# A four-stage network on one core: k's biases by a transfer of their own, padding zeroed by ScalarE, the recurrence's weights zeroed from the output bias

## The chip, the core and the metric

The kernel runs on one core of one Trainium2 chip. The metric is the time of one execution on the device in microseconds (us), the median of several runs. A profile of one execution lists every instruction with its engine, start and duration: PE (TensorE), DVE (VectorE), ACT (ScalarE), POOL (GpSimd) and SP (SyncE, which here only issues transfers). Line numbers are those of the kernel before.

## The reference, cut to what matters

The input x has shape (16, 512, 256). Four sublayers follow each other, each closed by a residual and a layer norm:

```python
x = layernorm(x + latent_attention(x))   # 16 heads of 16, latent size 32, rotary, causal softmax
x = layernorm(x + fp4_ffn(x))            # 256 -> 704 -> 256; activations and weights quantized
x = layernorm(x + recurrence(x))         # tanh state of 64 per head, 512 steps
x = layernorm(x + mix_ffn(x))            # token shift, sigmoid gate, squared relu

# inside latent_attention
qkv = x @ c_attn_w.T + c_attn_b
q_lat = rope(q @ q2l_w.T + q2l_b)
k_lat = rope(k @ kv2l_w.T + kv2l_b)
v_lat = v @ kv2l_w.T + kv2l_b
att = softmax(causal((q_lat @ wqk_w.T + wqk_b) @ k_lat.T * 32 ** -0.5))
y = (att @ v_lat) @ l2o_w.T + l2o_b
return y @ cproj_w.T + cproj_b
```

All values are float32.

## The kernel before, in words

The first two sublayers are computed together, batch by batch, for 16 batches; then the last two, token by token, in 512 steps. Only the start of the first batch matters here.

A preparation comes first. SP and ACT issue the transfers of weights. POOL makes constants: the identity, `mask` (L367, zeros with a triangle of large values), `ones`. The weights of the q and k heads are transposed by TensorE (L719) and copied into `wqk` (L725) in pieces, by whichever of ACT and VectorE the scheduler picks (`nc.any`). The heads of k are stacked with their two halves exchanged, so their biases are needed with the halves exchanged as well: that is `cabk` (L399), made by two small copies on VectorE.

`heads` (L442, L446) then makes q and k of batch 0, `latents` (L460 to L481) their rotated latents `qc` and `kc` and the product `qr`. In between, `output_weights` (L727 to L773) folds the value path, the output map and their biases into one matrix `wv` and one row `bo`, spread over all partitions: `turned_k`, `turned_o` (L737), `there` (L746), `wv` (L754), `by` (L765), `wide` (L766), `ps_bo` (L770, L771), `bo` (L772). POOL adds `bo` to the residual input of batches 0 and 1 (`load_residual`, L415, eight instructions).

`scores` (L527) makes the products S of a group of four heads, VectorE adds the mask and takes the row's extreme in one instruction (`p`, L539), ACT takes exponentials (L552), TensorE turns p (L562), ACT copies the turned p (L564). `values` (L424) makes v in a padded form, `vpad`: each head's 16 columns stand in 32, with zeros beside them. The zeros are written once, by POOL (L789), and the copies of L430 fill the rest, batch by batch. `weighted` (L593) multiplies.

Beside the attention of batch 0 the weights of the FP4 sublayer are quantized (`ffn_weights`, `fp4`): each tile is loaded by SP (L228) into one of two buffers, and then passes VectorE (L205 to L218, eight instructions) and POOL (L219, L220).

`recurrent_weights` (L109) prepares the third sublayer: it zeroes `wb` and `wc` on POOL (L116, L118), then places the blocks of the recurrence's weights in them by 16 and 4 small transfers (L132, L126), loads `ta` by 8 and takes its tanh on ACT (L135), loads four square matrices (L138) and `bout` (L140), which VectorE halves (L141). It is called in batch 2's turn of the loop, but the scheduler moves its instructions to the start, as nothing holds them.

The order on TensorE is the order in which the code calls it (`manual_schedule`). The order on every other engine and in SP's queue is the scheduler's: it follows priorities and the times at which it expects operands. Each engine runs its list strictly in order, and so does SP: an instruction that waits holds all behind it. Transfers use eight semaphores in turn, so each also waits for the transfer that had the same one.

Of the kernel before, what the change touches and what calls it, by code (L numbers as in the profile page):

```python
# [14 lines left out]
AF = mybir.ActivationFunctionType  # L15
ALU = mybir.AluOpType
# [3 lines left out]
P = 128  # L20
B, T, C = 16, 512, 256
NT = T // P
# [37 lines left out]
def tile_kernel(ctx: ExitStack, tc: tile.TileContext, I: dict, out: bass.AP):  # L60
    nc = tc.nc
# [11 lines left out]
    cols = const.tile([P, NCOLS], F32, name="cols")  # L73
# [32 lines left out]
    own = ctx.enter_context(tc.tile_pool(name="own", bufs=1))  # L106
    sq = {}

    def recurrent_weights():  # L109

        ta = own.tile([P, 2, 4, P], F32, name="ta")
        wb = own.tile([P, 4, 2, 2, P], F32, name="wb")
        nc.gpsimd.memset(wb, 0.0)  # L116
        wc = own.tile([P, 4, 2, 32], F32, name="wc")
        nc.gpsimd.memset(wc, 0.0)  # L118
        for par, quarters in enumerate(QUARTERS):
            for i, (r, c) in enumerate(quarters):  # L120

                e = i % 2
                of, rs, cs = slice(e * 64, e * 64 + 64), slice(r * 64, r * 64 + 64), slice(c * 64, c * 64 + 64)
                nc.sync.dma_start(ta[rs, par, :, cs], I["bda"][of, i // 2 :: 2, of])
                if par == 0:
                    nc.sync.dma_start(  # L126
                        wc[cs, :, r, c * 16 : c * 16 + 16],
                        I["bdc"][of, i // 2 :: 2, e * 16 : e * 16 + 16],
                    )
                for q2 in range(2):  # L130
                    at = slice(q2 * 64 + i * 16, q2 * 64 + i * 16 + 16)
                    nc.sync.dma_start(  # L132
                        wb[at, q2::2, par, r, cs], I["bdb"][at, q2 * 2 + i // 2 :: 4, of]
                    )
        nc.scalar.activation(ta, ta, AF.Tanh)  # L135
        for k in ("woutT", "wrT", "wkT", "wvT"):
            sq[k] = own.tile([P, 2, C], F32, name=k)
            nc.sync.dma_start(sq[k], I[k].rearrange("(n p) c -> p n c", p=P))  # L138
        bout = own.tile([P, C], F32, name="bout")
        nc.sync.dma_start(bout, I["bout"].to_broadcast([P, C]))  # L140
        nc.vector.tensor_scalar(bout, bout, 0.5, None, ALU.mult)  # L141
        return ta, wb, wc, bout
# [139 lines left out]
    def quantize_now(j):  # L282

        for _ in quantize(B - 1, j):
            vector_done(("x", B - 1, j))
# [60 lines left out]
    with ExitStack() as a:  # L346
# [8 lines left out]
        def load(b):  # L355
            xT_of[b] = xin.tile([P, 2, T], F32, tag="xT", name="xT")
            nc.sync.dma_start(xT_of[b], I["xT"][b].rearrange("(n p) t -> p n t", p=P))
# [8 lines left out]
        mask = wts.tile([P, T], F32, name="mask")  # L366
# [18 lines left out]
        bo = wts.tile([P, C], F32, name="bo")  # L385
# [5 lines left out]
        for i in range(2):  # L391
            nc.gpsimd.tensor_copy(bd["bdqs"][:, i::2], bd["bdq"][:, 1 - i :: 2])
            at = COLS["q2lb"][0]
            nc.sync.dma_start(q2lbs[i::2, :], I["cols"][1 - i :: 2, at : at + 1])

        cabk = wts.tile([P, 2], F32, name="cabk")
        for i in range(2):
            at = COLS["cab"][0] + 2
            nc.vector.tensor_copy(  # L399
                cabk[i * 64 : i * 64 + 64, :], cols[64 - i * 64 : 128 - i * 64, at : at + 2]  # L400
            )

        vpad = [wts.tile([P, NT, H, 32], F32, name=f"vpad{i}") for i in range(2)]
# [7 lines left out]
        def load_residual(b):  # L411
            x = xres.tile([P, NT, C], F32, tag="x", name="x")
            nc.sync.dma_start(x, I["x"][b * T : b * T + T, :].rearrange("(n p) c -> p n c", p=P))
            for j in range(NT):
                nc.gpsimd.tensor_tensor(x[:, j, :], x[:, j, :], bo, ALU.add)  # L415
            x_of[b] = x
# [102 lines left out]
        def scores(b, g, n):  # L519

            q, k = stack_of[b, g]
            S = [mm("S") for _ in range(4)]
            for i, at in BLOCKS[n]:
                w = (i + 1) * P
                for h in range(4):
                    rs = slice(h * 32, h * 32 + 32)
                    nc.tensor.matmul(  # L527
                        S[h][:, at : at + w], q[rs, i * P : i * P + P], k[rs, :w],
                        start=True, stop=True,
                    )  # L530
            if n == 0:
                sum_of[b, g] = small.tile([P, 2, 2, 4], F32, tag="sm", name="sm", bufs=3)
            tiles = []
            for h in range(4):
                p = pp.tile([P, T], F32, tag="p", name="p")
                nm = small.tile([P, 2], F32, tag="nm", name="nm", bufs=10)
                for u, (i, at) in enumerate(BLOCKS[n]):
                    own = slice(at, at + (i + 1) * P)
                    nc.vector.tensor_tensor_reduce(  # L539
                        out=p[:, own], in0=S[h][:, own], in1=mask[:, T - (i + 1) * P :],  # L540
                        scale=1.0, scalar=-MASKED, op0=ALU.add, op1=ALU.min,
                        accum_out=nm[:, u : u + 1],
                    )
                tiles.append((p, nm))
            return tiles

        def exponentials(b, g, n, h, p, nm):

            for u, (i, at) in enumerate(BLOCKS[n]):
                own = slice(at, at + (i + 1) * P)  # L550
                half, cb = PLACE[i]
                nc.scalar.activation(  # L552
                    p[:, own], p[:, own], AF.Exp, bias=nm[:, u : u + 1], scale=-1.0,
                    accum_out=sum_of[b, g][:, cb, half, h : h + 1],
                )
            return p

        def turn(n, p):
            w = sum(i + 1 for i, _ in BLOCKS[n]) * P
            ps = mm("ps_pt")  # L560
            for at in range(0, w, P):
                nc.tensor.transpose(ps[:, at : at + P], p[:, at : at + P], ident)  # L562
            pT = ptp.tile([P, T], F32, tag="pT", name="pT")
            nc.scalar.copy(pT[:, :w], ps[:, :w])  # L564
            return pT
# [220 lines left out]
        ps_y = five.enter_context(tc.tile_pool(name="ps_y", bufs=1, space=PSUM))  # L786
        banks[:] = [ps_2] * 2 + [ps_b] * 5
        for i in range(2):
            nc.gpsimd.memset(vpad[i], 0.0)  # L789

        with tc.manual_schedule(engines={mybir.EngineType.PE}):
            slots = [(b, g, n) for b in range(B) for g in range(4) for n in range(len(BLOCKS))]
            pTs, before, beside = [], None, None

            behind = []
            for slot in slots + [None]:
                if slot:
                    b, g, n = slot
                    if g == 0 and n == 0:
                        if beside:  # L800
                            beside.rest()
                        if b + 1 < B:
                            load(b + 1)
                        beside = Beside(b)
                        if b == 2:
                            ta, wb, wc, bout = recurrent_weights()
                    if g == 3 and n == 0:
                        load_residual(b)
                    tiles = scores(b, g, n)
                ps = []  # L810

                for h in range(4):
                    beside.half_slot()
                    if before:
                        pTs.append(turn(before[0][2], before[1][h]))
                    if slot:
                        behind.append((*slot, h, *tiles[h]))
                        ps.append(tiles[h][0])
                    while len(behind) > (LAG if slot else 0):
                        exponentials(*behind.pop(0))  # L820
                    if h == 1:
                        divide()
                    beside.half_slot()
                if before and before[0][2] == len(BLOCKS) - 1:
                    weighted(*before[0][:2], pTs)
                    pTs = []
                before = (slot, ps) if slot else None
            divide()
            last_projection = out_projection(B - 1)
            next(last_projection)  # L830
            quantize_now(0)
            next(last_projection)
# [297 lines left out]
    with tc.manual_schedule(engines={mybir.EngineType.PE}):  # L1130
# [40 lines left out]
        for t in range(T):  # L1171
# [9 lines left out]
            for g in range(2):  # L1181
                if us[g] is None or us[g][0] + us[g][1] == t:
                    t0, n = starts[g].pop(0)
# [9 lines left out]
            if t % 8 == 7:  # L1193
                at = t % 16 - 7
# [113 lines left out]
```

## Time and profile before

| what | value |
|---|---|
| runs | 2535.84, 2541.34, 2544.07 us |
| median | 2541.34 us |
| the profiled execution's time | 2540.61 us |
| its span, first to last instruction | 2538.8 us |
| mean granted TensorE clock | 0.982 of full speed |
| the recurrence's first product (L1029) starts at | 1813.2 us |

The profile's rows name the line, the engine, the operation, and output and inputs by the program's names. "Idle before" is the time for which the engine had nothing to run ahead of that instruction, with the instruction or transfer that ended the wait behind an arrow. The granted clock is the share of its full clock that TensorE was given in a stretch. The first ten microseconds are filled by transfers (249 GB/s in that stretch); TensorE starts at 6.1 us with the transposes.

### The profile page before, as it was taken

To read this page: it belongs to the slowest core of one execution; us is meant where nothing else is said; L and a number is where in the kernel's file an instruction comes from. 1 tells how busy PE (TensorE), PEld (TensorE's weight loads), DVE (VectorE), ACT (ScalarE), POOL (GpSimd) and SP (SyncE) were. 2 spreads that over 40 slices of the span, in tenths; PEclk is the share of its full clock that TensorE was granted. 3 is DMA by queue.
4 is the path that set the end of the run, shared out by engine and by line. 5 is a ranking of instruction groups with operands and counts; after the bars stand their busy time and mean duration, and the time that the engine had idled before them with its cause. 6 is when DMAs were issued, how large, how long until landed. Compare 5 with 4: busy or idle time off the path is not lost.

```text
span 2538.8 us, 73782 instructions
## 1 busy us (share of the span) xinstructions
PE 2405.2 (95%) x28802; PEld 1710.4 (67%) x28802; DVE 1925.8 (76%) x5479; ACT 1621.0 (64%) x5536; POOL 1044.4 (41%) x1646
## 2 busy tenths in 40 slices
PE   8789999999999999999999999987799999999997
PEld 4555666666666666666666666655578888888885
DVE  5767888788888888888888888877656666666666
ACT  4656666676766767666666666654366666666664
POOL 4323333333333333333333333333545555555554
PEclk9889999999999999999999999999899999999999
DMA  4000000000000000000000000000111111111100
GB/s 118 24 9 6 12 24 14 16 16 12 24 14 16 16 12 24 14 16 16 12 24 14 16 14 6 16 14 9 43 32 41 41 36 41 41 40 37 36 28 27
DMA packets 58015, 61.30 MB, mean 24 GB/s; under 512 B 7873, under 2 KB 53058, under 8 KB 57666
## 3 DMA queue, kind: packets, MB, share of 16 engines
q1 hardware_dynamic: 56802, 55.54, 7.0%
q8 instruction: 226, 3.70, 0.6%
q10 hardware_dynamic: 864, 1.05, 0.1%
q14 instruction: 123, 1.01, 0.1%
HBM read 39.79 MB, written 16.78 MB: 22 GB/s over the span
## 4 chain that ended last, share of the span: by engine, by line
PE 52%; DVE 28%; ACT 10%; POOL 5%; issue 4%; DMA 0%; DVEq 0%; POOLq 0%; ACTq 0%
PE u L1069 8%; DVE p L539 5%; PE ps_pt L562 5%; PE u L1029 5%; ACT p L552 4%; PE S L527 3%; PE ps_d L164 3%; DVE q_q L210 3%; PE pg L164 3%; PE pu L164 3%; PE ps_h L442 3%; ACT pT L564 3%; DVE q_q L218 2%; DVE q_sc L205 2%; PE ps_a L909 2%
## 5 line engine op out<-in xcount | busy, mean ns | idle before, releaser
L552 ACT ACTIVATE p<-p,nm 128x512 f32<-128x512 f32 (+3 forms) x1024 | 570.3, 562 | 492.0 <-DVE nm L539 488.0
L1077 ACT ACTIVATE hist<-u 64x64 f32<-64x64 f32 x2048 | 447.2, 218 | 233.9 <-PE u L1069 149.6
L539 DVE CUSTOM_DVE_ANT_0 p<-S,mask 128x512 f32<-128x512 f32 (+3 forms) x1024 | 442.7, 483 | 52.6 <-PE S L527 52.1
L562 PEld LDWEIGHTS ps_pt<-ident,p 128*128 128x128 f32 x2560 | 301.7, 142 | 217.0 <-issue 105.9
L1069 PEld LDWEIGHTS u<-hist,ta 128*64 128x64 f32 x8176 | 366.8, 138 | 118.6 <-ACT hist L1077 40.3
L564 ACT COPY pT<-ps_pt 128x384 f32<-128x384 f32 (+1 forms) x768 | 374.1, 517 | 58.0 <-PE ps_pt L562 57.8
L562 PE MATMUL ps_pt<-ident,p 128*128 128x128 f32 x2560 | 395.6, 280 | 4.7 <-DVE nm L539 3.3
L1069 PE MATMUL u<-hist,ta 128*64 128x32 f32 x8176 | 393.4, 218 | 4.6 <-ACT hist L1077 4.5
L219 POOL TENSOR_TENSOR q_q<-q_q,q_m 128x256 f32<-128x256 f32 (+1 forms) x142 | 166.7, 1174 | 368.5 <-DVE q_q L218 366.4
L527 PE MATMUL S<-kc,qr 32*128 32x512 f32 (+3 forms) x2048 | 223.9, 475 | 10.5 <-ACT qr L481 7.9
L1029 PE MATMUL u<-xt,wb 128*64 128x64 f32 x4128 | 224.6, 231 | 5.8 <-issue 5.2
L552 ACT ACTIVATION_READ_ACCUMULATOR p<-p,nm 128x1 f32 x1024 | 199.7, 195 | 0.0
L164 PE MATMUL ps_d<-wdT,hT 128*128 128x256 f32 x732 | 172.8, 386 | 13.7 <-DVE nm L539 12.1
L164 PE MATMUL pg<-wgT,xqT 128*128 128x352 f32 x512 | 177.2, 469 | 7.7 <-DVE nm L539 5.1
L476 POOL TENSOR_TENSOR qc<-qc,qs 128x512 f32<-128x512 f32 x64 | 81.5, 1274 | 232.1 <-DVE qs L475 217.7
L164 PE MATMUL pu<-wuT,xqT 128*128 128x352 f32 x512 | 174.6, 464 | 1.0 <-DVE nm L539 1.0
L1029 PEld LDWEIGHTS u<-xt,wb 128*64 128x64 f32 x4128 | 166.4, 140 | 10.6 <-issue 5.4
L593 PEld LDWEIGHTS py<-pT,vpad 128*32 128x32 f32 x5120 | 139.7, 110 | 47.2 <-issue 30.3
L593 PE MATMUL py<-pT,vpad 128*32 128x128 f32 x5120 | 164.0, 276 | 7.7 <-ACT pT L564 7.5
L164 PEld LDWEIGHTS ps_d<-wdT,hT 128*128 128x128 f32 x732 | 135.1, 191 | 37.1 <-DVE nm L539 15.4
L86 POOL TENSOR_SCALAR ve<-mv 128x2 f32<-128x2 f32 (+1 forms) x160 | 31.1, 195 | 311.7 <-DVE mv L94 309.0
L578 POOL COPY rcx<-rc 128x256 f32<-128x256 f32 x64 | 40.4, 631 | 287.3 <-DVE rc L576 259.5
(164 smaller groups left out, 4645.6 us busy)
## 6 DMA issues: line engine op xcount, KB each, us to landing
xT<-in_xT_dram SPq DMA_DIRECT2D x16, 512.0 KB
x<-in_x_dram SPq DMA_DIRECT2D x16, 512.0 KB
xs<-x SPq DMA_DIRECT2D x64, 128.0 KB
x<-xs SPq DMA_DIRECT2D x32, 256.0 KB
xm<-xs SPq DMA_DIRECT2D x32, 256.0 KB
out_dram<-o SPq DMA_DIRECT2D x64, 128.0 KB
w<-in_w_down_dram SPq DMA_DIRECT2D x2, 352.0 KB
w<-in_w_gate_dram SPq DMA_DIRECT2D x5, 128.0 KB
```

Source lines behind the costliest of these rows:

```text
L164: nc.tensor.matmul(dst, left, right, start=start, stop=stop)
L219: nc.gpsimd.tensor_tensor(q, q, m, ALU.subtract)
L476: nc.gpsimd.tensor_tensor(of[k], of[k], x, ALU.add)
L527: nc.tensor.matmul(S[h][:, at : at + w], q[rs, i * P : i * P + P], k[rs, :w], start=True, stop=True,)
L539: nc.vector.tensor_tensor_reduce(out=p[:, own], in0=S[h][:, own], in1=mask[:, T - (i + 1) * P :], scale=1.0, scalar=-MASKED, op0=ALU.add, ...
L552: nc.scalar.activation(p[:, own], p[:, own], AF.Exp, bias=nm[:, u : u + 1], scale=-1.0, accum_out=sum_of[b, g][:, cb, half, h : h + 1],)
L562: nc.tensor.transpose(ps[:, at : at + P], p[:, at : at + P], ident)
L564: nc.scalar.copy(pT[:, :w], ps[:, :w])
L593: nc.tensor.matmul(py[q * 32 : q * 32 + 32, PLACE[i][1], :], vpad[b % 2][:, j, g * 4 + h, :], pt, start=j == 0 and h % 2 == 0, stop=j == i ...
L1029: nc.tensor.matmul(u[rs, k, par:n:2, bs : bs + 16], wb[:, g * 2 + k, par, half, rs], xt[:, g, at : at + n - par : 2, :], start=par == 0 an ...
L1069: nc.tensor.matmul(into[cs, :, c, :], ta[:, t % 2, g * 2 + k, cs], own[:, :, c, :], start=False, stop=True, skip_group_check=True,)
L1077: nc.scalar.activation(state[g][rs, :, r * 32 : r * 32 + 32].rearrange("p k (s b) -> p k s b", s=2), u[rs, :, t - t0, :] .rearrange("p k ( ...
```

## The change

It has three parts. `cabk` is no longer copied from the loaded `cols` by VectorE, but loaded from memory by two transfers on SP. The zeros of `vpad` are written by ScalarE, as the mask times zero, instead of by POOL. `wb` and `wc` are zeroed on POOL still, but as the output bias `bo` times zero, so that this can't start before `bo` is there; the function gets `bo` for it.

```diff
-    def recurrent_weights():
+    def recurrent_weights(bo):
         ta = own.tile([P, 2, 4, P], F32, name="ta")
         wb = own.tile([P, 4, 2, 2, P], F32, name="wb")
-        nc.gpsimd.memset(wb, 0.0)
+        nc.gpsimd.tensor_scalar(
+            wb.rearrange("p a b c n -> p (a b c n)").rearrange("p (j n) -> p j n", n=C),
+            bo.unsqueeze(1).to_broadcast([P, 8, C]), 0.0, None, ALU.mult,
+        )
         wc = own.tile([P, 4, 2, 32], F32, name="wc")
-        nc.gpsimd.memset(wc, 0.0)
+        nc.gpsimd.tensor_scalar(wc.rearrange("p a b n -> p (a b n)"), bo, 0.0, None, ALU.mult)
...
         cabk = wts.tile([P, 2], F32, name="cabk")
         for i in range(2):
             at = COLS["cab"][0] + 2
-            nc.vector.tensor_copy(
-                cabk[i * 64 : i * 64 + 64, :], cols[64 - i * 64 : 128 - i * 64, at : at + 2]
+            nc.sync.dma_start(
+                cabk[i * 64 : i * 64 + 64, :], I["cols"][64 - i * 64 : 128 - i * 64, at : at + 2]
             )
...
         for i in range(2):
-            nc.gpsimd.memset(vpad[i], 0.0)
+            nc.scalar.activation(
+                vpad[i].rearrange("p j h d -> p j (h d)"), mask.unsqueeze(1).to_broadcast([P, NT, T]),
+                AF.Identity, scale=0.0,
+            )
...
-                            ta, wb, wc, bout = recurrent_weights()
+                            ta, wb, wc, bout = recurrent_weights(bo)
```

With it the scheduler lists some of the first instructions in another order. VectorE makes all eight pieces of `wqk`, `turned_o` and `there`; it runs `qc`, `kc`, `by`, `wide`, `qs` and `ks` ahead of the quantization of the third and fourth weight tile, and that ahead of the first `p`; it halves `bout` ahead of the second group's `qc` and `kc`. POOL's list has `wb` behind the eight additions of `bo` and the third tile's L219, and `wc` behind the fourth's. SP's list has the two `cabk` transfers behind `q2lbs`, the transfers of `ta` ahead of the fifth weight tile, and those of `wc` and `wb` last, behind `bout`. TensorE's list is unchanged.

## The prediction

> **What bounds the kernel now.** I read the page first: the span, the busy shares and the chain that ended last.
>
> ```profile
> span 2538.8 us, 73782 instructions
> PE 2405.2 (95%) x28802; PEld 1710.4 (67%) x28802; DVE 1925.8 (76%) x5479; ACT 1621.0 (64%) x5536; POOL 1044.4 (41%) x1646
> PE 52%; DVE 28%; ACT 10%; POOL 5%; issue 4%; DMA 0%; DVEq 0%; POOLq 0%; ACTq 0%
> ```
>
> TensorE is busy 95% of the span and is over half of the chain. The order of instructions on each engine, before against after, differs only before the second block of softmax work, some 45 us into the span; from there on all five engines run the same list. So the change is worth what it does to the first 45 us, and I read those next, by stages:
>
> ```profile
> 16.20:26.30 10.10, 7.50 (x40) 4.59 (x38) 8.81 (x29) 1.59 (x4) 4.21 (x7) 1.00 0.36 97
> 26.40:36.60 10.20, 9.33 (x19) 3.02 (x20) 2.98 (x9) 4.12 (x11) 7.82 (x10) 0.50 0.21 42
> 36.70:46.70 10.00, 10.00 (x50) 5.85 (x50) 4.45 (x13) 6.88 (x18) 0.00 (x0) 1.00 0.54 162
> ```
>
> The columns are length, busy time of PE, PE's loads, DVE, ACT and POOL, then the granted clock. From 26.4 to 36.6 us TensorE had half its clock. The timeline says why, and names what the change touches:
>
> ```profile
> 3.34 6.06 DVE L399 COPY cabk<-cols 64x2 f32<-64x2 f32 x2
> 3.64 3.56 POOL L789 MEMSET vpad<- 128x2048 f32 x2
> ...
> 7.13 1.81 POOL L116 MEMSET wb<- 128x2048 f32 x1
> ...
> 9.61 0.23 DVE L379 TENSOR_SCALAR w<-w 128x128 f32<-128x128 f32 x1 [0.22 <-DMA w<-in_bdw_dram]
> 9.76 1.20 DVE L725 COPY wqk<-ps_t 128x128 f32<-128x128 f32 x5
> ...
> 11.01 3.78 PE L442 MATMUL ps_h<-xT,wqk 128*128 128x512 f32 x4 [2.95 <-DVE wqk L725]
> ...
> 25.43 1.11 PE L770 MATMUL ps_bo<-cpT,wide 128*128 128x256 f32 x4 [2.12 <-issue]
> ...
> 28.70 5.52 POOL L415 TENSOR_TENSOR x<-x,bo 128x256 f32<-128x256 f32 x8
> ...
> 32.64 0.69 DVE L539 CUSTOM_DVE_ANT_0 p<-S,mask 128x512 f32<-128x512 f32 x1 [5.80 <-PE S L527]
> ```
>
> Each row is start, duration, engine and instruction, then the idle time before it and what ended it. VectorE's tiny cabk copies take 6.06 us while POOL fills vpad and wb; yet VectorE's next instruction waits for w's DMA until 9.61. Later PE idles 2.12 us before ps_bo, because `wide` (L766) stands on VectorE behind the quantization of weight tiles three and four.
>
> **The change, part by part.** All times are worked against the profiled execution: span 2538.8, time 2540.61 us, 1.8 outside the span; that is 0.73 under the median of the three runs (2541.34).
>
> *The cabk copies become transfers.* This takes 6.06 us from VectorE, but w's transfer, issued at 3.16 ahead of the two new ones, still lands at 9.6: VectorE gains its 0.22 of idle at most, nothing on the path. On SP the two narrow transfers stand behind q2lbs; two of that kind took 1.50 us with a wait in them, wb's 0.6 each. Each SP transfer also waits for the one eight places before it, so two more shift every such pairing: cawv now waits for sin (landed about 9.5) instead of cos (8.5) and goes at 9.7 for 8.51; the first weight tile goes at about 11.2 for 10.28. The DMA engines are 0.8 busy to 20 us with the same bytes in the same order, so I take the landings as moved by 0 to 0.9 us, 0.3 likely (first tile 14.2 to 14.5). cabk itself leaves by 9.7 and is used at 17.0: even the 4.1 us of bout (40.74 issued, 44.84 used) leaves 3 us of cover.
>
> *vpad zeroed by ScalarE.* It adds two activations of 128x2048 on ACT. L1014's 128x1024 takes 1.04; between 1.7 and 2.1 each, so some 4 us. ACT is free from its table load (ends 5.55) to its first `heads` at 14.83: hidden with over 4 us to spare. Without that cover the price would be 4 us. In exchange the three L725 copies that ACT made go to VectorE (eight copies, 9.8 to 11.6), but the second is now the last half of the block that PE's first `heads` product needs: PE starts at about 10.35 instead of 11.01. turned_o (0.37) and `there` (0.26) go from ACT to VectorE too, behind the first two tiles' quantization: I put turned_o at 16.2, `there` at 18.0, ps_w at 18.1 (18.61 before): gain 0.5, range 0 to 0.7.
>
> *What VectorE does next.* qc, kc, by, `wide`, qs and ks now stand ahead of tiles three and four. ps_q to ps_ks take PE as long as before, to 22.8. VectorE takes the third tile's maximum at 20.6, after POOL's first wq, qc to 21.6, the fourth maximum at 22.1 (POOL's second wq), kc to 23.2, by and wide 0.6 more: PE's ps_bo at 23.8 instead of 25.43, an idle gap of 1.0 for 2.12. qs and ks end at 25.15. So far the change is 1.6 us ahead.
>
> *What that pushes back.* Tiles three and four (eleven VectorE instructions, some 2.7 us alone) now run after ks and ahead of the first p (L539), while POOL adds qc, kc (1.27 each) and the eight x+bo (0.69 each): continuous from 24.65. Before, they ran in 20.6 to 24.1, mostly with POOL idle. What such an overlap costs is seen later in this trace:
>
> ```profile
> 63.09 1.28 POOL L476 TENSOR_TENSOR qc<-qc,qs 128x512 f32<-128x512 f32 x1 [2.31 <-DVE qs L475]
> ...
> 63.52 0.99 DVE L214 TENSOR_SCALAR q_m<-q_q 128x256 uint32<-128x256 uint32 x1
> ...
> 64.32 1.33 POOL L476 TENSOR_TENSOR kc<-kc,ks 128x512 f32<-128x512 f32 x1
> 64.55 1.25 DVE L215 TENSOR_SCALAR q_m<-q_m 128x256 f32<-128x256 f32 x1
> ```
>
> Undisturbed, L214 and L215 take 0.29. Each ends just after the POOL addition beside it. [...] By price tags alone the first p could start when S is ready, about 29 to 31; by the rule nine of the eleven wait: two behind qc and kc, seven alternating with x+bo. That gives 27.5 after kc, then seven times (0.69 + about 0.28): the first p at 34.4, against 32.64: 1.8 later.
>
> *wb and wc.* They leave POOL's start, where nothing waited for them but the copies, and stand after x+bo and tile three: x+bo to 35.1, q_q 0.74, wb from 35.85. A POOL tensor_scalar of 128x2048 isn't in the trace. Below: the fill it replaces, 1.81. Above: the two-input addition, 1.27 for 512, so 5.1. Nearest: L872's 0.482 for 256 and L86's 0.195 for 2 give 1.13 ns an element, so 2.5; I take 2.5. VectorE's bout scaling (L141), now ahead of qc and kc of the next group, is of the kind that waits: p ends 36.85, wb 38.35, bout 38.6, qc 39.3. PE's ps_v needs that bank: 39.3 instead of 40.34. The next p (128x384) starts at 39.95 instead of 40.35. On SP the transfers of wb and wc wait for wc's fill, some 39 us, and hold back xT of batch 2 from 44.5 to about 51 (20 issues of 0.6); it is used after 140 us. bout's transfer, behind the fifth tile's, leaves at 31.5 and has landed by 36. ta's tanh (1.06) no longer waits at 38.98. POOL ends wc near 39.6, before its next qc.
>
> *The sum.* Between 0.4 (VectorE, ACT) and 1.0 us (PE) ahead at 40 us, kept to the end since all that follows is the same list: 0.7 faster. On the profiled execution 2539.9, on the median 2540.6.
>
> *The clock* is the unknown. [...] by the row, staying fast would give ps_qf 1.2, S 1.0, ps_h 1.8: 4.0 us. But with p at 34.4 PE has nothing to do from about 31.6 until p frees a bank, 3 us, and then loses the clock there and some 2 us on ps_v. I book none of it and let the range carry minus 4 to plus 2.
>
> **The rivals.**
> - *Faster: POOL does not hold VectorE.* If the tail passes x+bo at its own 2.7 us, p starts at 28.6 and PE stays fast: S 27.6, ps_v 34.1 instead of 40.34: 6.2 us, 2535. For it: the rule and rows show pairs, not a chain of eight. Against: the 0.99 and 1.25. Beyond 0.3% it needs one or two half-clock stretches of the first batch (1.7 us each) to go as well.
> - *Slower: wb's fill holds bout.* Up to 3.5 us for wb, ps_v still comes at 40.3; each us more delays bout, qc and ps_v by one. At 5.1 that is 1.6 late, with the clock lost at 31.6 to 35 another 2.2: 2545. For it: cabk's 6.06 us shows a wait over several POOL instructions. Against: 2.5 is the nearest price.
> - *It does nothing:* the 6.06 us were hidden by w's landing, the rest cancels: 2541.
>
> **How the numbers follow.** The three runs before span 8.2 us, 0.3%; a difference below that can't be told from none. My case, with "nothing", 0.66, all within 0.3%; faster rival 0.20, of which 0.16 beyond 2533.7; slower rival 0.14, of which 0.10 beyond 2549. Range: 2533 to 2548, from the rival's 2535 less 2 of scatter to 2545 plus 3.
>
> **What would show it.** Right: ps_bo near 23.8 with under 1.2 us idle before it; L214 to L218 of tiles three and four at 0.7 to 1.0 each beside x+bo; first p at 33.5 to 35; bout's scaling ending with wb. Wrong: first p before 31, or a wb over 4 us, or a different rate anywhere after 60 us.

## The result and the profile after

The changed kernel is slower: 2545.95 us (median of 22 runs, 2542.42 to 2549.74) against 2542.31 us for the kernel before beside it (22 runs). The ratio is 1.0015, 95% interval 1.0009 to 1.002: 3.6 us. In a second set of runs it was 2544.93 (13 runs) against 2541.13, ratio 1.0012 (1.0003 to 1.002). The prediction had 0.7 us faster. The profiled execution took 2546.28 us. Line numbers from here on are those of the changed kernel: from the transfers into `wb` and `wc` up to the zeros of `vpad` they are four higher than before, behind those eight.

The page with its chain that ended last, and then the three stages that were shown of before (length, busy time of PE, its loads, VectorE, ScalarE and POOL, granted clock, and the transfers' share and GB/s):

```profile
span 2544.5 us, 73778 instructions
PE 2406.0 (95%) x28802; PEld 1712.0 (67%) x28802; DVE 1933.7 (76%) x5482; ACT 1623.9 (64%) x5533; POOL 1042.9 (41%) x1644
PE 51%; DVE 29%; ACT 10%; POOL 5%; issue 4%; DMA 1%; SPq 0%; ACTq 0%; DVEq 0%; POOLq 0%
```

```profile
16.20:26.30 10.10, 7.58 (x40) 4.48 (x38) 9.38 (x29) 1.43 (x3) 3.30 (x5) 1.00 0.64 183
26.40:36.60 10.20, 8.90 (x27) 2.85 (x25) 10.16 (x20) 4.46 (x10) 10.20 (x12) 0.83 0.37 113
36.70:46.70 10.00, 6.78 (x26) 4.72 (x27) 7.43 (x11) 5.03 (x15) 5.60 (x3) 0.83 0.06 8
```

The totals say little: one point of the chain went from PE to VectorE. The stages say where. From 26.4 to 36.6 us TensorE now has 0.83 of its clock where it had half, and runs 27 matmuls where it ran 19. From 36.7 to 46.7 it is busy 6.78 us where it was busy all 10, and the clock that was full is 0.83. The loss is in that last stage. The timeline of the changed kernel up to the first p:

```profile
9.70 0.23 DVE L383 TENSOR_SCALAR w<-w 128x128 f32<-128x128 f32 x1 [6.43 <-DMA w<-in_bdw_dram]
...
11.54 0.94 SPq L232 DMA_DIRECT2D w<-in_w_gate_dram  x2
16.18 0.42 DVE L209 TENSOR_REDUCE q_sc<-w 128x16 f32<-128x256 f32 x1 [4.42 <-DMA w<-in_w_gate_dram]
...
19.63 1.16 PE L754 MATMUL ps_w<-there,cawv 128*128 128x128 f32 x8 [0.97 <-DVE there L750]
...
24.91 1.10 PE L774 MATMUL ps_bo<-cpT,wide 128*128 128x256 f32 x4 [0.58 <-issue]
...
28.46 6.26 POOL L419 TENSOR_TENSOR x<-x,bo 128x256 f32<-128x256 f32 x8
29.44 0.81 DVE L219 TENSOR_SCALAR q_m<-q_m 128x256 f32<-128x256 f32 x1
...
33.37 0.68 DVE L543 CUSTOM_DVE_ANT_0 p<-S,mask 128x512 f32<-128x512 f32 x1
```

The first row shows VectorE idle for 6.43 us before w lands: the 6.06 us that the cabk copies held it have become idle time. The next two show the first weight tile issued 1.3 us and used 2.0 us later than before (10.28 and 14.20). Then comes the place where it is decided, in the changed kernel and, below it, the same matmul and the same halving of bout in the kernel before:

```profile
35.38 5.38 POOL L117 TENSOR_SCALAR wb<-bo 128x2048 f32<-128x2048 f32 x1
...
35.82 5.09 DVE L145 TENSOR_SCALAR bout<-bout 128x256 f32<-128x256 f32 x1
...
40.83 0.73 DVE L474 SCALAR_TENSOR_TENSOR qc<-ps_q,cols,cos 128x512 f32<-128x512 f32 x1
...
41.62 2.89 PE L428 MATMUL ps_v<-wv,xT 128*128 128x256 f32 x8 [3.01 <-DVE qc L474]
```

```profile
40.27 1.99 PE L424 MATMUL ps_v<-wv,xT 128*128 128x256 f32 x8
...
40.74 0.47 SPq L140 DMA_DIRECT2D bout<-in_bout_dram  x1
...
44.84 0.29 DVE L141 TENSOR_SCALAR bout<-bout 128x256 f32<-128x256 f32 x1 [2.49 <-DMA bout<-in_bout_dram]
...
45.95 0.75 DVE L475 SCALAR_TENSOR_TENSOR qs<-ps_qs,q2lbs,sin 128x512 f32<-128x512 f32 x1 [0.82 <-PE ps_ks L460]
```

Read the first of them from the bottom. PE stood idle 3.01 us before ps_v, and qc on VectorE ended that wait. qc came straight behind bout's halving, 256 elements per partition that take 0.29 us in the kernel before and here 5.09. The halving ends just after POOL's fill of wb. And ps_v takes 2.89 us for the 1.99 of before: the granted clock is 0.50 from 42.6 to 46.0 us, in the stretch that follows the wait. The starts of the same matmul in the two traces, compared, give PE's position against the kernel before: 2.70 us ahead at 36.3 us, 1.35 behind at the first ps_v, 3.03 behind at 43 us and still 3.03 behind at 80 us.

### The profile page after: what moved, and what is told of

Its sections match the earlier page's. It is cut to its first block, busy times and chain, and to the rows that moved or that the text cites. A ratio compares the mean times of both kernels' runs of the same rounds, so it can differ in the third digit from the quotient of the medians.

```text
span 2544.5 us, 73778 instructions
## 1 busy us (share of the span) xinstructions
PE 2406.0 (95%) x28802; PEld 1712.0 (67%) x28802; DVE 1933.7 (76%) x5482; ACT 1623.9 (64%) x5533; POOL 1042.9 (41%) x1644
## 4 chain that ended last, share of the span: by engine, by line
PE 51%; DVE 29%; ACT 10%; POOL 5%; issue 4%; DMA 1%; SPq 0%; ACTq 0%; DVEq 0%; POOLq 0%
PE u L1077 8%; DVE p L543 5%; PE ps_pt L566 5%; PE u L1037 5%; ACT p L556 4%; PE ps_d L168 3%; PE S L531 3%; DVE q_q L214 3%; PE pg L168 3%; PE pu L168 3%; ACT pT L568 3%; DVE q_q L222 2%; DVE q_sc L209 2%; PE ps_a L917 2%; PE ps_h L446 2%
## 5 line engine op out<-in xcount | busy, mean ns | idle before, releaser
L1077 PEld LDWEIGHTS u<-hist,ta 128*64 128x64 f32 x8176 | 366.9, 138 | 118.8 <-ACT hist L1085 40.8
L223 POOL TENSOR_TENSOR q_q<-q_q,q_m 128x256 f32<-128x256 f32 (+1 forms) x142 | 166.6, 1174 | 375.0 <-DVE q_q L222 369.9
L86 POOL TENSOR_SCALAR ve<-mv 128x2 f32<-128x2 f32 (+1 forms) x160 | 31.1, 194 | 313.2 <-DVE mv L94 310.5
```

The lines of the kernel that those rows point to most:

```text
L223: nc.gpsimd.tensor_tensor(q, q, m, ALU.subtract)
L1077: nc.tensor.matmul(into[cs, :, c, :], ta[:, t % 2, g * 2 + k, cs], own[:, :, c, :], start=False, stop=True, skip_group_check=True,)
```

## The experiments

Every kernel was timed beside the kernel before. Position is that of PE at 60 us against the profile of before (plus is behind), worked out from the starts of the same matmul in the two traces; each is from a single profiled execution, and not all of these are typical. Those of wb, wc by memset and of parts 1 and 3 alone were the slowest of their runs, 5.7, 7.4 and 5.4 us above their medians; that of cabk on ScalarE's queue was the third fastest of 21, 3.6 below. So a position shows where time went in one execution, and the ratio says how much it is worth. The kernel before itself stood at 2541.13, 2540.51 and 2542.96 us in the three sets of runs; times that were expected in us are to be read against that.

| kernel | median us (runs) | before beside it | ratio, 95% interval | first ps_v | position |
|---|---|---|---|---|---|
| changed kernel | 2545.95 (22) | 2542.31 | 1.0015, 1.0009 to 1.002 | 41.62 | +3.03 |
| changed kernel, again | 2544.93 (13) | 2541.13 | 1.0012, 1.0003 to 1.002 | 40.96 | +3.28 |
| bout halved by ScalarE | 2538.71 (13) | 2541.13 | 0.9992, 0.9984 to 1.0 | 38.98 | -1.29 |
| fill in another form | 2539.80 (21) | 2542.96 | 0.999, 0.9983 to 0.9996 | 37.86 | -2.41 |
| wb, wc by memset | 2543.24 (21) | 2541.13 | 1.0009, 1.0002 to 1.0016 | 39.63 | +5.78 |
| the same, bout loaded early | 2539.85 (13) | 2540.51 | 0.9994, 0.9986 to 1.0002 | 40.50 | +0.23 |
| part 1 alone (cabk transfers) | 2543.46 (22) | 2540.51 | 1.0012, 1.0005 to 1.0018 | 40.72 | +6.79 |
| part 2 alone (vpad on ScalarE) | 2541.04 (13) | 2542.96 | 0.9992, 0.9984 to 1.0 | 39.52 | -0.76 |
| part 3 alone (wb, wc from bo) | 2544.91 (22) | 2540.51 | 1.0015, 1.0009 to 1.0021 | 44.07 | +6.56 |
| cabk copied by VectorE | 2539.89 (13) | 2541.13 | 0.9998, 0.999 to 1.0006 | 41.03 | +0.77 |
| cabk on ScalarE's queue | 2543.76 (21) | 2542.96 | 1.0001, 0.9994 to 1.0007 | 39.60 | -0.67 |
| cabk copied, bout by ScalarE | 2537.90 (22) | 2540.51 | 0.9989, 0.9983 to 0.9996 | 39.61 | -0.66 |
| the best of these | 2540.07 (21) | 2542.96 | 0.9987, 0.998 to 0.9993 | 38.02 | -2.24 |

The theory after the first profile: wb's fill on POOL holds bout's halving on VectorE, qc and ps_v wait behind it, and the clock goes. The rivals: the later weight tile costs, or the loss is made after 130 us, where the profiles of after and before drift apart by another 4 us.

**The changed kernel again.**

> The changed kernel once more, beside the kernels of this set. Theory (wb's fill on POOL holds bout on VectorE, so qc and ps_v come late and TensorE loses its clock there): wb's fill 5.2 to 5.6 us, bout's scaling ends with it, ps_v near 41.6 with an idle of about 3 us before it, and the time 3 to 4.3 us above the kernel before. Between 136 and 250 us the first profile of it lost another 4 us to the clock; if that belongs to the run and not to the kernel, that part of the shift differs here by 2 us or more. Rival (the loss is made there, after 130 us): the same +4 between 136 and 250 us again.

The fill took 5.38 us again and bout 5.09, with 3.01 idle before ps_v at 40.96: it is no accident of one run. Between 136 and 250 us it drifted from 3.8 to 5.6 behind, less than the first profile (3.6 to 6.4) and short of the difference of 2 expected. So the drift did not go away in a second execution; how much of it is the kernel's own is not settled.

**bout on ScalarE.**

```diff
-        nc.vector.tensor_scalar(bout, bout, 0.5, None, ALU.mult)
+        nc.scalar.activation(bout, bout, AF.Copy, scale=0.5)
```

> bout halved by ScalarE and not by VectorE; all else as in the changed kernel, wb's fill from bo too. Theory (wb's fill does no harm but by holding bout on VectorE): wb's fill keeps its 5.4 us, bout on ScalarE takes 0.3 to 0.5, qc ends by 37 and ps_v starts at 37.5 to 39.2; 2541 to 2543. Rival A (the first weight tile's later landing costs): 2545 to 2546. Rival C (any VectorE instruction behind bout that reads SBUF is held by the fill just as well, and the wait only moves to qc): qc takes 3 us or more beside the fill, ps_v at 41 again, 2545 to 2546.

The lists of TensorE, POOL and SP are unchanged; one instruction moves from VectorE to ScalarE. Its timeline:

```profile
35.53 5.37 POOL L117 TENSOR_SCALAR wb<-bo 128x2048 f32<-128x2048 f32 x1
...
35.95 0.74 DVE L474 SCALAR_TENSOR_TENSOR qc<-ps_q,cols,cos 128x512 f32<-128x512 f32 x1
...
37.12 0.40 ACT L145 ACTIVATE bout<-bout 128x256 f32<-128x256 f32 x1
...
38.98 1.99 PE L428 MATMUL ps_v<-wv,xT 128*128 128x256 f32 x8
```

The fill is as long as ever, qc and ScalarE's bout run beside it at their normal pace, and the whole loss is gone: the ratio goes from 1.0012 to 0.9992 beside the same runs of before. The first weight tile still came at 16.12. So the later tile does not cost by itself (rival A falls), and the fill does not hold everything on VectorE (rival C falls). Beside it qc and p, which read one of their inputs from PSUM, passed at 0.74 and (128x384) 0.54; bout on VectorE, from SBUF to SBUF, took 5.09 in the changed kernel. What in the instructions makes this difference is not shown.

**The fill in another form.** What L880 does: two operations in one instruction, the first factor from a column.

```diff
+        zero = own.tile([P, 1], F32, name="zero")
+        nc.gpsimd.memset(zero, 0.0)
...
-            bo.unsqueeze(1).to_broadcast([P, 8, C]), 0.0, None, ALU.mult,
+            bo.unsqueeze(1).to_broadcast([P, 8, C]), zero[:, :1], 1.0, ALU.mult, ALU.mult,
...
-        nc.gpsimd.tensor_scalar(wc.rearrange("p a b n -> p (a b n)"), bo, 0.0, None, ALU.mult)
+        nc.gpsimd.tensor_scalar(wc.rearrange("p a b n -> p (a b n)"), bo, 0.0, 1.0, ALU.mult, ALU.mult)
```

> The changed kernel with wb's fill in another form of the same POOL operation, the one that L880 uses (factor taken from a column of zeros, then times 1.0), and wc's fill with a second immediate factor of 1.0; every engine runs the same list but for a memset of one column. L880 takes 0.523 us for 128x256. Theory F (the fill's 5.38 us comes from its form, and the hold is worth what the fill lasts): wb's fill 2.3 to 3.2 us, bout ends with it near 38.5, ps_v at 38.5 to 39.6 for 41.6, the idle before it under 1 us; 2540 to 2542.5, 2.5 us or more off the changed kernel. Rival G (any POOL multiplication of 2048 elements by a number costs this): fill at 5.2 to 5.6, ps_v near 41.3, 2544 to 2546. wc shows by itself whether the second immediate factor matters: 0.5 for 0.84 if so.

```profile
34.73 1.97 POOL L117 TENSOR_SCALAR wb<-bo,zero 128x2048 f32<-128x2048 f32 x1
35.14 1.71 DVE L145 TENSOR_SCALAR bout<-bout 128x256 f32<-128x256 f32 x1
...
36.77 0.73 DVE L474 SCALAR_TENSOR_TENSOR qc<-ps_q,cols,cos 128x512 f32<-128x512 f32 x1
37.40 0.41 POOL L122 TENSOR_SCALAR wc<-bo 128x256 f32<-128x256 f32 x1
...
37.86 1.99 PE L428 MATMUL ps_v<-wv,xT 128*128 128x256 f32 x8
```

This is the cleanest of the runs: every engine runs the same list, but for POOL's memset of the column, and wb's fill is 3.4 us shorter, more than the 2.2 to 3.1 expected. bout still ends with it, ps_v keeps its clock, and the time goes from 0.12 to 0.15% above the kernel before to 0.10% below it. That is some 6 us for 3.4 us of fill. The second profile of the changed kernel shows how: at 36.3 us the two executions are level (4.91 and 4.93 us ahead of the kernel before), from 43 us on they are 5.7 apart. ps_v starts 3.1 us later there (40.96 for 37.86), and TensorE then has half its clock from 39.4 to 46.2 us, which makes the rest. Here it keeps full clock:

```profile
36.70:46.70 10.00, 9.67 (x59) 6.46 (x60) 5.59 (x15) 6.56 (x18) 3.42 (x4) 1.00 0.11 14
```

wc, with a second factor of 1.0 and no column, fell from 0.84 to 0.41, so for it the second operation alone is enough.

**wb and wc by memset again.**

```diff
-        nc.gpsimd.tensor_scalar(
-            wb.rearrange("p a b c n -> p (a b c n)").rearrange("p (j n) -> p j n", n=C),
-            bo.unsqueeze(1).to_broadcast([P, 8, C]), 0.0, None, ALU.mult,
-        )
+        nc.gpsimd.memset(wb, 0.0)
...
-        nc.gpsimd.tensor_scalar(wc.rearrange("p a b n -> p (a b n)"), bo, 0.0, None, ALU.mult)
+        nc.gpsimd.memset(wc, 0.0)
```

> wb and wc zeroed by plain memsets again, the two other parts kept. Theory (wb's fill holds bout): POOL fills wb before its first quantization, bout goes behind p, qc no longer waits, ps_v starts at 37.5 to 39.2 for 41.6 and keeps its clock; 3 to 4.5 us less than the changed kernel: 2541 to 2543, at or below the kernel before. Rival A (the two cabk transfers, which brought the first weight tile 2.0 us later, are what costs): the first tile still lands at 16.2, and the time stays at 2545 to 2546. Rival B (the loss comes after 130 us from how the clock's stretches fall): anything from 2543 to 2549, with no tie to where ps_v starts.

ps_v came at 39.63 (37.5 to 39.2 expected) at full clock (its eight in 1.99 us), but the time came down by only 1.7 of the 3.8 us, which the intervals do not tell from none. The timeline, that of the slowest of its 21 runs, shows a wait that had not been there:

```profile
43.90 0.47 SPq L144 DMA_DIRECT2D bout<-in_bout_dram  x1
...
49.13 0.29 DVE L145 TENSOR_SCALAR bout<-bout 128x256 f32<-128x256 f32 x1 [8.83 <-DMA bout<-in_bout_dram]
49.34 0.74 DVE L479 SCALAR_TENSOR_TENSOR qs<-ps_qs,q2lbs,sin 128x512 f32<-128x512 f32 x1
...
50.14 2.31 PE L531 MATMUL S<-kc,qr 32*128 32x256 f32 x14 [1.58 <-DVE qs L479]
```

With early fills the small transfers into wb and wc go out early, ahead of bout's, and bout's leaves SP at 43.90; in the changed kernel, where they wait for the fill, it left at 31.22. It is the same instruction again: bout's halving, now waiting for its transfer, with qs behind it. In the kernel before it left at 40.74, and qs behind the halving still had 0.82 us to wait for PE: that was all the cover it had.

**Memsets, and bout loaded early over ScalarE's queue.**

```diff
-        nc.sync.dma_start(bout, I["bout"].to_broadcast([P, C]))
+        nc.scalar.dma_start(bout, I["bout"].to_broadcast([P, C]))
```

> wb and wc zeroed by memsets, and bout loaded by a transfer on ScalarE's queue at the start, so that VectorE halves it in the first 10 us; the two other parts as in the changed kernel. With the memsets alone, bout's transfer left SP at 43.9, landed at 49.1, and VectorE stood 8.8 us before it with qs behind. Theory (that wait is where the memsets' gain went): the gap of PE before S near 50 us goes, PE is 0.5 to 1.5 us ahead of the kernel before at 60 us where it was 5.8 behind: 2538 to 2540.5. Rival A (the first tile's lateness costs): 2542 to 2543.5, as with the memsets alone.

bout was halved at 10.42 us, the gap before S went, and the ratio fell from 1.0009 to 0.9994: the wait on the transfer was where the memsets' gain had gone. PE at 60 us was level (0.23 behind), not the 0.5 to 1.5 ahead that were expected.

**Each part alone,** put on the kernel before. First part 1:

```diff
-            nc.vector.tensor_copy(
+            nc.sync.dma_start(
-                cabk[i * 64 : i * 64 + 64, :], cols[64 - i * 64 : 128 - i * 64, at : at + 2]
+                cabk[i * 64 : i * 64 + 64, :], I["cols"][64 - i * 64 : 128 - i * 64, at : at + 2]
```

> The kernel before with the two cabk transfers alone (vpad, wb and wc zeroed by POOL's memsets as before). The first weight tile should land at 15.3 to 16.3 for 14.2, and the transfer of bout, last of SP's row of small ones, should leave 2 to 3 us later than 40.74 and land at 47 to 49 for 44.8. Theory (whatever VectorE's halving of bout waits for is what costs: POOL's fill in the changed kernel, the transfer here): qs stands behind it on VectorE and had only 0.82 us to spare, so qs and S come 1.5 to 3.5 us late near 48 us: 2543 to 2545. Rival A (the late first tile costs by itself, about 1 us at ps_w, and bout nothing): 2541 to 2542.5.

```profile
44.91 0.47 SPq L140 DMA_DIRECT2D bout<-in_bout_dram  x1
...
50.14 0.29 DVE L141 TENSOR_SCALAR bout<-bout 128x256 f32<-128x256 f32 x1 [7.33 <-DMA bout<-in_bout_dram]
50.35 0.74 DVE L475 SCALAR_TENSOR_TENSOR qs<-ps_qs,q2lbs,sin 128x512 f32<-128x512 f32 x1
```

Two transfers of 64 by 2 numbers cost 3 us. In the execution shown, the slowest of 22, it was not by the late tile: PE was level (0.45 behind) at ps_v, and 6.8 behind at 60 us. bout's transfer left 4.2 us later than before, and it landed at 50.1, more than the 47 to 49 expected. No run here loads bout early with part 1 alone; that this wait is what part 1 costs rests on this trace and on the pair of runs above.

Then part 3, the change's own lines for wb and wc:

```diff
-        nc.gpsimd.memset(wb, 0.0)
+        nc.gpsimd.tensor_scalar(
+            wb.rearrange("p a b c n -> p (a b c n)").rearrange("p (j n) -> p j n", n=C),
+            bo.unsqueeze(1).to_broadcast([P, 8, C]), 0.0, None, ALU.mult,
+        )
...
-        nc.gpsimd.memset(wc, 0.0)
+        nc.gpsimd.tensor_scalar(wc.rearrange("p a b n -> p (a b n)"), bo, 0.0, None, ALU.mult)
```

> The kernel before with wb and wc filled from bo alone (cabk copied by VectorE, vpad by POOL's memsets). wb's fill 5.2 to 5.6 us, from 33.5 to 35 us on; bout's halving now stands before the fourth p and is held to the fill's end, near 39.5 to 40; ps_v at 40.8 to 42. Theory (the hold costs wherever it is): 1 to 4 us over the kernel before: 2542 to 2545. Rival D (the hold costs only together with the later tiles of part 1, as cabk copied by VectorE already brought the time to 2539.9 with the hold in place): 2540 to 2541.5.

```profile
35.06 5.38 POOL L117 TENSOR_SCALAR wb<-bo 128x2048 f32<-128x2048 f32 x1
35.28 0.69 DVE L543 CUSTOM_DVE_ANT_0 p<-S,mask 128x512 f32<-128x512 f32 x1
35.89 4.69 DVE L145 TENSOR_SCALAR bout<-bout 128x256 f32<-128x256 f32 x1
...
40.51 0.67 DVE L543 CUSTOM_DVE_ANT_0 p<-S,mask 128x512 f32<-128x512 f32 x1
```

The hold is there without the two other parts, with the fourth p behind it as well, and the change costs 4.4 us. ps_v came at 44.07, past the 40.8 to 42 expected; this execution, too, was the slowest of 22. The third p, which reads S from PSUM, ran beside the fill at 0.69.

And part 2:

```diff
-            nc.gpsimd.memset(vpad[i], 0.0)
+            nc.scalar.activation(
+                vpad[i].rearrange("p j h d -> p j (h d)"), mask.unsqueeze(1).to_broadcast([P, NT, T]),
+                AF.Identity, scale=0.0,
+            )
```

> The kernel before with vpad zeroed by ScalarE alone (cabk copied by VectorE, wb and wc by POOL's memsets as before). cabk's copies now have one fill of 1.8 us beside them and end near 5.5; the first weight tile lands as before at 14 to 14.7. Theory (the loss lies in what VectorE's halving of bout waits for): bout leaves SP as before near 41, lands near 45, nothing waits for it; the time within 1.5 us of the kernel before, 2539 to 2542. Rival H (the third and fourth tile's instructions, moved behind ks and beside POOL's eight x+bo, delay the first p): first p at 34 or later, 2542 to 2544.

vpad on ScalarE alone does no harm: 0.9992, at the edge of what can be told from none. The first p came at 33.10, not at 34. So parts 1 and 3 cost 3.0 and 4.4 us alone, part 2 gained 1.9, and all three together cost about 3.7. That is less than the sum, 5.5, but the intervals are too wide to say that the parts do not add up. The traces give two reasons why they need not. Parts 1 and 3 act on one instruction: with wb's fill late, the small transfers no longer stand ahead of bout's (it left at 31.22 in the changed kernel), so SP's delay does not reach it, and the hold takes its place. And the scheduler's lists are not sums of each other: with part 1 or part 2 alone VectorE has five instructions of the weight tiles between ks and the first p, in the changed kernel eleven.

**cabk by other ways.** First by VectorE again, as in the kernel before, the rest as in the changed kernel; then by transfers on ScalarE's queue.

```diff
-            nc.sync.dma_start(
-                cabk[i * 64 : i * 64 + 64, :], I["cols"][64 - i * 64 : 128 - i * 64, at : at + 2]
+            nc.vector.tensor_copy(
+                cabk[i * 64 : i * 64 + 64, :], cols[64 - i * 64 : 128 - i * 64, at : at + 2]
```

```diff
-            nc.sync.dma_start(
+            nc.scalar.dma_start(
                 cabk[i * 64 : i * 64 + 64, :], I["cols"][64 - i * 64 : 128 - i * 64, at : at + 2]
             )
```

> cabk copied by VectorE again, vpad on ScalarE and wb, wc filled from bo as in the changed kernel. With no vpad fill on POOL beside them the two copies should take 0.1 to 0.4 us each. Theory (wb's fill holds bout): the first weight tile lands near 14.3, PE is 1 to 1.5 us earlier up to 36 us, but wb's fill starts only some 1 us earlier and still holds bout, ps_v at 40 to 41.3: 2544 to 2545.5, that is at most 2 us of the 3.6. Rival A (the tile's late landing is what costs): 2541.5 to 2543.

> The changed kernel with the two cabk transfers issued by ScalarE's queue and not by SP's. Theory (they cost by their place on SP's queue, ahead of the weight tiles): the first tile lands at 14 to 15 for 16, and the time comes to that of the kernel with cabk copied by VectorE, 2539 to 2541.5, though wb's fill still holds bout for some 5 us. Rival I (cabk's copies were the better place for another reason; the hold alone costs the 3.6): 2543.5 to 2545.5.

With no fill beside them the two copies took 0.55 us, and the tile came at 14.45. But the time fell further than the theory allowed, and further than rival A, to 0.9998 with the fill still there:

```profile
34.79 5.38 POOL L117 TENSOR_SCALAR wb<-bo 128x2048 f32<-128x2048 f32 x1
35.21 5.12 DVE L145 TENSOR_SCALAR bout<-bout 128x256 f32<-128x256 f32 x1
...
41.03 1.13 PE L428 MATMUL ps_v<-wv,xT 128*128 128x256 f32 x4 [1.59 <-DVE qc L474]
```

In that execution TensorE had half its clock from 24.4 to 34.6 us, so its work reached further into the hold: it idled 1.59 us for 3.01, kept the clock, and was 0.77 behind where the changed kernel was 3.03. That half the clock falls there in every execution of it can't be told from one profile. Nor is the tile the only other difference: with the copies, VectorE again has only five instructions of the tiles between ks and the first p, and POOL has two of the x+bo behind the fourth tile's L223. What of the gain belongs to which is open. The hold's cost depends on what stands before it.

On ScalarE's queue the tile did not come back: 16.11, a miss. w's transfer waited 3.4 us on SP for bdk, one of the transfers of ScalarE's queue:

```profile
3.57 1.41 ACTq L403 DMA_DIRECT2D cabk<-in_cols_dram  x2
5.53 0.34 SPq L382 DMA_DIRECT2D w<-in_bdw_dram  x1
```

Both queues draw on the same eight semaphores, so two more transfers shift the pairing on either: in the order of issue over both queues w is the eleventh here and waited for the third, bdk; in the kernel before it is the ninth and waited 1.0 us for the first, cols. The time was still level with the kernel before beside it (1.0001), though its 2543.76 us lies in rival I's range. In the profiled execution, with the lists ordered as with the copies, POOL was late enough that bout's halving slipped in ahead of the fill and took 0.81 (35.59, fill from 36.96). That execution took 2540.14 us, while the 21 runs spread from 2538.26 to 2551.42; whether the halving falls behind the fill in the slower ones is not shown.

**Versions that keep what helped.** First the changed kernel with the edits of two runs above, cabk's copies by VectorE and bout on ScalarE; then, of all edits above, vpad on ScalarE as in part 2, the memsets for wb and wc, cabk copied by VectorE, and bout loaded early. The cut shows the last two against the changed kernel.

```diff
-        nc.sync.dma_start(bout, I["bout"].to_broadcast([P, C]))
+        nc.scalar.dma_start(bout, I["bout"].to_broadcast([P, C]))
...
-            nc.sync.dma_start(
-                cabk[i * 64 : i * 64 + 64, :], I["cols"][64 - i * 64 : 128 - i * 64, at : at + 2]
+            nc.vector.tensor_copy(
+                cabk[i * 64 : i * 64 + 64, :], cols[64 - i * 64 : 128 - i * 64, at : at + 2]
             )
```

> The changed kernel with cabk copied by VectorE and bout halved by ScalarE, both at once. Theory (hold and late transfers each cost, and add up): first tile near 14.4, qc not held, ps_v at 37.5 to 39.5 for 41.0; 1.5 to 4 us below the kernel with the copies alone: 2536 to 2538.5, clearly faster than the kernel before. Rival D (once the tiles are early the hold is covered): 2539 to 2541, the same as with the copies alone.

> A version that takes what the runs so far favour: vpad zeroed by ScalarE, wb and wc by early memsets on POOL, cabk copied by VectorE while it waits for w, and bout loaded over ScalarE's queue at the start. Theory: first tile at 14.3 to 15.3, no wait on bout anywhere, PE at 60 us 0.5 to 2 us ahead of the kernel before; 2536.5 to 2539, level with cabk's copies and bout on ScalarE (2537.9). Rival J (the later ps_bo of the early tiles eats it, as PE then waits 2 us for wide): 2539.5 to 2541.

Both are faster than the kernel before, by 0.11% and 0.13%. Against the copies alone (0.9998, up to 1.0006), bout on ScalarE (0.9989, from 0.9983) takes off some 2.3 us more, within what the two intervals leave open: the hold may cost there too, but less than in the changed kernel. The best of these, at 2540.07, missed the 2536.5 to 2539 expected, lies in rival J's range and is no better than the single change of the fill's form (0.999) by more than the intervals allow.

## Why the prediction was wrong

*The price of wb's fill* is the step that failed. The sum had 2.5 us for it, 5.1 as the most; the fill took 5.38, above that bound, and 5.37 with no halving of bout beside it. The wait itself, bout behind the fill and qc and ps_v behind bout, was forecast rightly; its size was not. Both rows that gave the price were of another form: L872 (L880 in the changed kernel) multiplies twice in one instruction, L86 multiplies and adds, and the fill multiplies once. POOL has no tensor_scalar with a single operation anywhere in the kernel before, so no row could show what that form costs. In the form of L880 the fill takes 1.97 and the time falls below that of before. With a fill of 2.5 the change would by that have been a gain; no run has that length.

*The slower rival named the wait, and was partly lucky with its number.* Its delay of ps_v, 1.6 us at a fill of 5.1, was 1.35 in the first profile. But it put the loss of the clock at 31.6 to 35 us, ahead of the first p. There TensorE had full clock from 32.3 us on; it had half from 42.6 to 46.0, behind the fill, and from 39.4 to 46.2 in the second profile. So the 2545 came out of the right wait and of a clock loss at another place. It was given 0.14, because the price was taken from the nearest rows and their form was not compared with the fill's. The 3 us without work for PE that the paragraph on the clock expected before the first p were not there either: in the first profile PE ran ps_h from 31.08 us and ps_q from 33.59.

*What halves the clock* is not shown, in the kernel before or in any run here. There the half clock from 26.4 us came behind the gap of 2.12 ahead of ps_bo; but behind a longer one, 2.95 ahead of ps_h at 11.01, the clock was full up to 20 us. In the changed kernel the gap ahead of ps_bo was 0.58, and the clock was half from 28.9 us all the same. That PE without work would lose its clock, and that a shorter gap would spare it, were the author's estimates.

*The tile's landing* was put at 14.5 with 14.2 to 15.1 as range; it was 16.18, and 15.51 in the second profile. Its issue moved by 1.26 us (10.28 to 11.54), and from issue to use it took 4.64 us for 3.92. This moved ps_w from the 18.1 forecast to 19.63 and ps_bo from 23.8 to 24.91, yet bout on ScalarE was fast with the tile at 16.12.

*What held.* The copies' 6.06 us would otherwise have been idle: VectorE waited 6.43 for w. vpad's two activations took 3.71 us and nobody waited; PE's heads started at 10.51 (10.35 forecast). ps_bo's idle was 0.58, under the 1.2 named. Of the eleven instructions of tiles three and four behind ks, eight (nine were forecast) took 0.64 to 1.19 us each beside POOL's additions, for 0.13 to 0.42 in the kernel before with POOL idle (20.6 to 23.1 us). The rule that the sum went by is that of its rows at 63 us, where two such instructions ended just after POOL's; that nine of the eleven would wait was the author's estimate. The first p came at 33.37, one us earlier than the 34.4 of the sum. The other effect left unbooked, a faster clock from 26 to 36 us, was there: with half clock only from 28.9 to 32.3 us PE was 2.7 us ahead at 36.3, with full clock throughout in the second profile 4.9, and gave it all back behind the fill.

*What was costed at nothing too lightly.* Part 1 was given 0 to 0.9 us on the landings, and bout's transfer was followed only in the changed order. That qs behind it had 0.82 us to spare in the kernel before was to be read in its trace (the row at 45.95 above), and is what part 1 alone runs into.

*Still open.* PE's lag grew from about 3 us at 80 us to about 6 at the end in both profiles, while the medians differ by 3.6 to 3.8. Some 1.7 us of that is the measure: the profiled execution of the kernel before took 2540.61 us, that much under its median. With bout's halving on ScalarE it is a lead that grew, from 1.3 us at 80 us to 5.3 at 260, and was 2.8 at the end. The stretches of half clock between 80 and 260 us fall differently in the profiles, and no run here holds them still.

## What to carry to other kernels

An unimportant instruction in an ordered list is as urgent as what stands behind it. bout is not needed for 1.8 ms, yet its halving on VectorE, held by a POOL fill, made the changed kernel some 3.7 us slower, and in the kernel with the memsets, held by a late transfer, it ate the gain. Giving it to another engine cured the first, loading it earlier the second. When a price is taken from a near row, compare the two instructions' forms field by field, operations and factors, before the element count; where no row has the form, the range has to be wide. And before adding up what parts cost alone, ask which one instruction each of them delays, and whether the scheduler still lists the same order.

## What the runs showed of the hardware

On POOL, tensor_scalar with one multiplication by a number took 5.38 us for 128x2048 and 0.84 for 128x256; with a second multiplication by 1.0 it took 1.97 (first factor from a column) and 0.41 (first factor a number). The instruction with more to do was the faster; why is not shown.

VectorE's tensor_scalar from SBUF to SBUF, the halving of bout, ended just after POOL's fill however long that was (5.09, 4.69 and 5.12 us beside a fill of 5.38, 1.71 beside one of 1.97, for 0.29 in the kernel before), while VectorE's instructions with an input in PSUM ran beside it at 0.74 (qc) and 0.69 (p), and ScalarE halved bout beside it in 0.40.

A transfer on one queue held one on another, where the program gives both the same semaphore: with two transfers of 64 by 2 numbers added to ScalarE's queue, w's on SP waited 3.4 us for bdk's of ScalarE's queue, eight places before it, and was issued at 5.53 us for 3.11.
